# The last two sure expert steps add their rows up in PSUM by one-hot products, with the branch last, values from two spans and idle products at the start

## The chip, the cores and the metric

The kernel runs on one core of a Trainium2 chip. The metric is device time in microseconds (us) of one execution, the median of three runs. The profile is of one further execution, taken by the hardware profiler; its times are counted from the first instruction of the program. Engines are named as the profile names them: PE (TensorE, the matmuls; PEld its weight loads), DVE (VectorE), ACT (ScalarE), POOL (GpSimd) and SP (SyncE, which here only issues DMAs).

## What is computed

Two decoder layers on `x` of 4 sequences, 256 tokens, 256 features, with a context of 4 x 1601 rows, in float32. After each of six blocks the input is added and the sum goes through a layer normalisation.

```python
x = ln(x + L0_attention(x))        # 16 heads of 16, sliding window: 64 queries see 2 x 64 keys
x = ln(x + L0_cross(x, ctx))       # keys: 1601 of the context and the 256 tokens themselves
x = ln(x + L0_ffn(x))              # ternary weights, activations rounded to 8 bits
x = ln(x + L1_attention(x))        # causal, 16 heads, low-rank keys and values
x = ln(x + L1_cross(x, ctx))       # linear attention over the context
x = ln(x + L1_ffn(x))              # 8 experts, 2 per token
```

The last one concerns the end of the kernel:

```python
logits = 30 * tanh(x @ w_gate / 30); weights = softmax(logits), kept for the top 2 of 8 experts
for e in range(8):
    out += (silu(x @ w1[e]) * (x @ w3[e])) @ w2[e] * weights[:, e]
```

The first one concerns its start: each block of 64 queries sees its own 64 keys and the 64 before them, as far as these lie at a distance of 0 to 64.

## The kernel before, in words

**How the order is made.** The kernel doesn't issue instructions directly. Every call on `k` (a `Loom`) records an operation with an estimated cost per engine; a `piece` is a group of matmuls that stays together. At the end `weave()` (L317) is a list scheduler: it takes, over and over, the operation that can start first by its model, and emits it, so each engine has a fixed order in the finished program. Buffers belong to rings (`Group`), PSUM is one ring of eight banks (`psB`, tag `bank`), and a buffer comes free by the model's time. A change of one operation can thus move others on all engines. All DMAs of plain form go through SP in one order.

**The start.** SP loads the first sequence's `xT`, the query, key and value weights (`wqkv`) and the context of sequence 2. POOL meanwhile builds the identity, ones, the window mask `wmask`, the head mask `hmask` and two value buffers `v` (filled with zeros). `hmask` gives `qmask`, by which the keys are scaled.

**The first attention (`l0_attention`, L681).** Per sequence: products for keys and queries, then values in three spans of 128 tokens, at 0, 64 and 128 (`for i in range(3)`, L693), each two products of 128x256 whose outcome DVE and ACT copy into `v[:, i]`, the even and the odd heads. Tokens 0 to 127 as queries use span 0, tokens 128 to 191 span 1, tokens 192 to 255 span 2. `unit(j)` (two per sequence) makes scores for eight heads, adds the mask on DVE, takes the softmax on DVE and ACT (`softmax`, L643), turns the outcome on PE and multiplies by `v`. Between these the scheduler places matmuls of `context_sums`, which belong to the second layer's cross attention.

**The experts.** `route` picks two experts per token and POOL scatters the token's row, with its weight and its place, into a list per expert in DRAM (`lists`, filled with zeros before that by six DMAs in `moe_prepare`, L1231). `tile_table` works out on the core which 128 rows of which expert are the next tiles. An expert step, `expert_tile` (L1413), reads 128 rows (`xg`), loads that expert's `w1` and `w3`, turns the rows, makes 16 products for both matrices, applies the gate and makes four products with `w2` into `py`. DVE scales `py` to `y`, and POOL scatters the 128 rows of `y` to the DRAM array `yd`, which has two rows per token (`scatter`, L1262).

There are 23 tiles at most. 20 are always run; the last three (`RARE`) stand in a branch, `rare_tiles` (L1478), which is entered only if the tokens spread so that more tiles are needed. In the profiled execution it isn't. The branch stands after the sure steps and before the end. After it, per sequence, SP reads two blocks of `yd` back (`back`, a ring of four), DVE adds both to `x`, `normalise` (L614) takes statistics on DVE, the root on POOL and the scaling on DVE, and SP stores the sequence to `out` (L1576 to L1584).

Of the kernel before, what the change touches and what calls it, by code (L numbers as in the profile page):

```python
# [31 lines left out]
P = 128  # L32
# [105 lines left out]
class Pool:  # L138
# [3 lines left out]

    def tile(self, shape, dtype, tag, name=None, bufs=None, free=False, acc=False):
        if self.scope.loom.at_once is not None:
            return self.scope.loom.at_once[tag].pop(0)
        g = self.groups.get(tag)
        if g is None:
            g = self.groups[tag] = Group(self, tag, bufs or self.bufs, free)
        b = Buf(g, list(shape), dtype, name or tag, acc)
        self.scope.bufs.append(b)  # L150
        return View(b, None, shape)
# [281 lines left out]
def decoder(ctx: ExitStack, tc: tile.TileContext, a: dict, out: bass.AP):  # L433
# [44 lines left out]
    def tiny(shape, tag, dtype=F32):  # L478
        return small.tile(shape, dtype, tag, free=True)
# [70 lines left out]
    for b in range(1, B):  # L550
        load_x(b)
        load_res(b)

    ident = const.tile((P, P), F32, "ident")
    k.op({"POOL": (1.2, 1.2, lambda: make_identity(nc, ident.real()))}, [ident], [])
    identb = const.tile((P, P), BF16, "identb")
# [9 lines left out]
        )  # L566

    wmask = p1w.tile((P, 2, P), F32, "wmask")
    lower = p1.tile((P, 2, 2, P), F32, "at", bufs=7)[:, 0, 0]
    k.gpsimd.memset(wmask, 0.0)
    k.gpsimd.memset(lower, 0.0)
    for m, off in ((wmask[:, 0], 0), (wmask[:, 1], 64), (lower, 0)):
        keep_where(m, [[-1, P]], off, 1, NEG)
        keep_where(m, [[1, P]], 64 - off, -1, NEG)
    k.vector.tensor_copy(wmask[64:, 1], lower[64:])
# [7 lines left out]
    for par in range(2):  # L586
# [3 lines left out]
            axis=AX.X,  # L590
        )
    k.vector.tensor_scalar(qmask, qmask, 0.25, None, ALU.mult)


    vs = []
# [85 lines left out]
    def l0_attention(b):  # L681
# [20 lines left out]
        oT = pool.tile((P, 2, S), F32, "oT1", bufs=1)  # L702

        def unit(j):
# [512 lines left out]
    EARLY[1] -= EARLY[0]  # L1217
    TILES = 2 * T // P + NE - 1
    LATE = TILES - sum(EARLY)
    RARE = NE // 2 - 1  # L1220
    LISTS = (NE + 1) * T
    W = D + 2
# [8 lines left out]
    def moe_prepare():  # L1231
        pool, n = p5w, LISTS // P
        blank = p3.tile((P, FF), F32, "h")[:, :W]
        k.gpsimd.memset(blank, 0.0)
        for i in range(0, n, 12):
            dst = lists[i * P : (i + 12) * P, :].rearrange("(n p) w -> p n w", p=P)
            filled.append(k.dma_start(dst, blank.unsqueeze(1).to_broadcast([P, 12, W]), after=loaded))
        places = pool.tile((P, T // P, 2), F32, "places")
# [17 lines left out]
    filled, entered, taken_up, made = [], [], [], []  # L1256

    def apart(new, others):
        for o in others:
# [150 lines left out]

    tables = []

    def expert_tile(i, tab, level):  # L1413
        pool = p6
        reg = {}

# [46 lines left out]
        with piece(1.75, [y], ins=[w2], what="tile"):  # L1463
            for c in range(4):
# [2 lines left out]
                    c == 0, c == 3,  # L1467
                )
        k.also = [k.vector.tensor_scalar(y, py, gate, 0.5, ALU.mult, ALU.mult)]
        slots = p5.tile((P, 1), I32, "slots")  # L1470
# [7 lines left out]
    def rare_tiles(tiles, tab, more, level):  # L1478

        spare = [  # L1480
            p5.tile((P, W), F32, "xg"), p6w.tile((P, 2, 2, EI), F32, "wt"), p6.tile((P, 2, P), F32, "xgT"),
            p6.tile((P, EI // P, P), F32, "eh"), p6.tile((P, D), F32, "ey"), p5.tile((P, 1), I32, "slots"),
        ]
        banks = [bank((P, 2, P)), bank((P, EI // P, P)), bank((P, EI // P, P)), bank((P, D))]

        def emit():
            k.hold_order(False)
# [2 lines left out]
            for arm in tc.Switch(which, 2):  # L1490
                if arm:
                    for i in tiles:
                        k.at_once = {v.buf.group.tag: [v] for v in spare}
                        k.at_once["bank"] = list(banks)
                        expert_tile(i, tab, level)
                        k.at_once = None
            k.hold_order(True)

        k.op({None: (0.0, 2.5, emit)}, [yd], [tab, more, w2], [*spare, *banks], after=[o for o in k.ops if o.bufs], unordered=True)


    for b in range(B):
# [67 lines left out]
        X[b] = xn  # L1570
    at_prio(8)
    tab, more = tile_table(LATE, taken, True)
    for i in range(LATE - RARE):
        expert_tile(i, tab, level)
    rare_tiles(range(LATE - RARE, LATE), tab, more, level)
    for b in range(B):  # L1576
        x = X[b]
        for e in range(2):
            y = p6.tile((P, 2, D), F32, "back", bufs=4)
            row0 = 1 + e * T + b * S  # L1580
            k.dma_start(y, yd[row0 : row0 + S, :].rearrange("(t p) d -> p t d", p=P))
            k.vector.tensor_tensor(x, x, y, ALU.add)
        normalise(x)
        k.dma_start(out[b * S : (b + 1) * S, :].rearrange("(t p) d -> p t d", p=P), x)  # L1584
    k.weave()


# [69 lines left out]
```

## Time and profile before

| | us |
|---|---|
| median of three runs (lowest, highest) | 696.57 (695.5, 697.3) |
| the profiled execution | 696.37 |
| its span, first to last instruction | 694.7 |
| PE busy | 646.5 (93%) |
| DVE busy | 441.5 (64%) |
| ACT busy | 294.3 (42%) |
| POOL busy | 123.4 (18%) |
| DMA: read and written | 83.53 MB, mean 120 GB/s |

A busy share is that of an engine over the whole span, and matmuls overlap each other, so it doesn't say what a stage waits for. For that one reads a stage's own lines. In a line of the timeline the columns are the start, the length, the engine, the line of the code (a helper's, mostly), the operation, the tiles written and read, the number of instructions merged, and in brackets how long the engine had been idle and what released it. A record of PE is half a product in float32: two records stand for one 128x256 product.

### The profile page before, as it was taken

The numbers are of one execution on the slowest core, as the hardware profiler recorded it, in microseconds if no ns is written. First come the engines' busy times: TensorE is split into PE (matmuls) and PEld (weight loads), VectorE is DVE, ScalarE is ACT, GpSimd is POOL, SyncE is SP. The second block draws the span as 40 slices with busy tenths as digits, with TensorE's granted clock in tenths as the row PEclk, the third lists the DMA queues.
The fourth block names the chain that finished last, engine by engine and source line by source line (L and its number), as shares of the span: only waits on it lengthen the run. The fifth ranks groups of instructions, "written<-read, shape, count | busy, mean of one in ns | idle before, by whom it ended". The sixth has DMA issues, their size and how long they took to land.

```text
span 694.7 us, 12093 instructions
## 1 busy us (share of the span) xinstructions
PE 646.5 (93%) x4281; PEld 514.7 (74%) x4285; DVE 441.5 (64%) x1141; ACT 294.3 (42%) x924; POOL 123.4 (18%) x167
## 2 busy tenths in 40 slices
PE   7999999999999999999999999999997899999950
PEld 5787878668877777776667677777775799899940
DVE  5878897333527654374599997776688375333326
ACT  2767965211132433344346777656456312111100
POOL 3313223013300000000022101141203022111112
PEclk9999999999999999999999999999999899999985
DMA  9922100636998322000020330000000681996315
GB/s 303 357 83 77 41 31 1 212 93 231 330 300 293 122 95 94 1 1 0 1 55 1 105 139 1 1 30 1 31 1 23 218 288 43 330 308 235 116 45 168
DMA packets 60480, 83.53 MB, mean 120 GB/s; under 512 B 4462, under 2 KB 43764, under 8 KB 60404
## 3 DMA queue, kind: packets, MB, share of 16 engines
q1 hardware_dynamic: 58676, 77.86, 34.0%
q0 software_dynamic: 1728, 4.74, 1.9%
q8 instruction: 38, 0.62, 0.4%
q14 instruction: 38, 0.31, 0.2%
HBM read 67.29 MB, written 15.29 MB: 119 GB/s over the span
## 4 chain that ended last, share of the span: by engine, by line
PE 66%; DVE 14%; issue 11%; ACT 4%; POOL 3%; DMA 2%; SPq 0%; POOLq 0%; DVEq 0%
PE bank L269 58%; PE bank L276 8%; DVE at L406 4%; ACT at L406 3%; DVE nm L406 2%; POOL yd L1267 2%; DVE x L406 1%; DVE h L406 1%; POOL rstd L406 1%; DVE as L406 1%; DVE entry L406 1%; DVE st L406 1%; DMA yd<-ey,slots 1%; DVE kf L406 0%; DMA back<-yd 0%
## 5 line engine op out<-in xcount | busy, mean ns | idle before, releaser
L406 ACT ACTIVATE at<-at,nm 128x128 f32<-128x128 f32 (+1 forms) x256 | 106.5, 420 | 25.7 <-DVE nm L406 25.2
L269 PE MATMUL bank<-xgT,wt 128*128 128x128 f32 x640 | 75.9, 279 | 1.4 <-DMA wt<-in_w 0.9
L269 PEld LDWEIGHTS bank<-xgT,wt 128*128 128x128 f32 x640 | 75.1, 195 | 2.5 <-issue 1.3
L276 PE MATMUL bank<-ident,at 128*128 128x128 f32 (+1 forms) x440 | 61.4, 277 | 1.8 <-DVE at L406 1.6
L276 PEld LDWEIGHTS bank<-ident,at 128*128 128x128 f32 (+1 forms) x440 | 51.0, 142 | 13.8 <-issue 5.7
L269 PE MATMUL bank<-V,aT 128*128 128x256 f32 (+1 forms) x240 | 55.2, 380 | 0.7 <-DVE o L406 0.7
L269 PE MATMUL bank<-KT,qT 128*128 128x512 f32 (+1 forms) x128 | 54.0, 553 | 0.0
L269 PEld LDWEIGHTS bank<-V,aT 128*128 128x128 f32 (+1 forms) x240 | 45.2, 190 | 11.2 <-issue 3.6
L406 POOL TENSOR_SCALAR rstd<-mv 128x2 f32<-128x2 f32 (+1 forms) x26 | 6.5, 250 | 264.3 <-DVE mv L406 218.7
L269 PE MATMUL bank<-kf,V 128*128 128x256 f32 (+1 forms) x208 | 50.4, 383 | 1.1 <-DVE kf L406 1.1
L406 DVE TENSOR_REDUCE nm<-at 128x4 f32<-128x512 f32 (+1 forms) x64 | 50.7, 808 | 0.4
L269 PE MATMUL bank<-wkv,KT 128*128 128x256 f32 (+1 forms) x208 | 49.7, 382 | 0.0
L406 ACT ACTIVATION_READ_ACCUMULATOR at<-at,nm 128x1 f32 x256 | 48.8, 191 | 0.0
L406 ACT COPY aT<-bank 128x512 f32<-128x512 f32 (+2 forms) x60 | 31.4, 552 | 30.2 <-PE bank L276 29.5
L269 PEld LDWEIGHTS bank<-kf,V 128*128 128x128 f32 (+1 forms) x208 | 38.2, 190 | 7.5 <-DVE kf L406 2.3
L269 PEld LDWEIGHTS bank<-wkv,KT 128*128 128x128 f32 (+1 forms) x208 | 37.8, 186 | 7.3 <-issue 1.5
L406 ACT ACTIVATE eh<-bank 128x512 f32<-128x512 f32 x20 | 11.9, 597 | 67.9 <-PE bank L269 60.0
L406 DVE TENSOR_TENSOR at<-at,rs 128x512 f32<-128x512 f32 (+1 forms) x43 | 39.8, 925 | 0.8
L406 POOL TENSOR_TENSOR at<-at,rs 128x512 f32<-128x512 f32 (+1 forms) x21 | 23.5, 1121 | 86.9 <-DVE rs L406 73.6
L269 PE MATMUL bank<-w2e,eh 128*128 x160 | 37.8, 380 | 0.0
L406 ACT ACTIVATE fm<-bank 128x512 f32<-128x512 f32 (+2 forms) x33 | 18.1, 552 | 46.1 <-PE bank L269 46.1
L406 DVE TENSOR_REDUCE m<-bank 128x1 f32<-128x512 f32 (+1 forms) x32 | 20.5, 640 | 25.8 <-PE bank L269 25.6
(247 smaller groups left out, 1215.3 us busy)
## 6 DMA issues: line engine op xcount, KB each, us to landing
wt<-in_w SPq DMA_DIRECT2D x40, 512.0 KB
lists<-h SPq DMA_DIRECT2D x6, 1548.0 KB
KT<-in_ctxT SPq DMA_DIRECT2D x6, 1024.0 KB
V<-in_ctx SPq DMA_DIRECT2D x6, 1024.0 KB
w2e<-in_w SPq DMA_DIRECT2D x8, 512.0 KB
KT<-in_ctxT SPq DMA_DIRECT2D x6, 577.0 KB
V<-in_ctx SPq DMA_DIRECT2D x6, 512.0 KB
xg<-lists SPq DMA_DIRECT2D x20, 129.0 KB
```

What stands on the lines that cost most here:

```text
L269: lambda: self.nc.tensor.matmul(real(o), real(lhsT), real(rhs), start=real(start), stop=stop, **kw)
L276: fns.append(lambda: self.nc.tensor.transpose(real(o), real(x), real(ident)))
L406: return getattr(engine, method)(*[real(x) for x in args], **{k: real(x) for k, x in kw.items()})
L1267: d = nc.gpsimd.indirect_dma_start(out=dst.real(), out_offset=bass.IndirectOffsetOnAxis(ap=row.real(), axis=0), in_=src.real(), in_offset= ...
```

## The change

It has five parts.

1. **Idle products.** At the very start DVE writes a tile of zeros (from the ring of `qT`), PE makes eight bf16 products of 128x512 from it into a bank that nobody reads, and ACT takes an Exp of one column of it.
2. **Masks.** `hmask` and `qmask` are built before `wmask`. The second half of `wmask` is for swapped halves of the keys.
3. **Values from two spans.** Only the spans at tokens 0 and 128 are multiplied. `v[:, 1]` is put together from half of each: rows 64 to 127 of the first span and rows 0 to 63 of the second. Each span is thus copied twice, once whole and once in half, by DVE and by ACT. Scores for the queries 128 to 191 are made in two halves of 64 keys each, swapped likewise.
4. **Clearing.** `moe_prepare` fills the first 2048 token rows of `yd` with zeros by two more DMAs, because rows that are no longer scattered are still read.
5. **The end.** The last two of the 20 sure steps don't scatter. DVE compares the place of each row with a ramp of 1024 numbers (`iotaT`, made on POOL) and gets a one-hot tile `pick`; eight products per step, two per sequence, add the rows of `y` to four PSUM banks `acc`, one per sequence. The rest is read back from `yd` once the other 18 steps have scattered, added to `x` as before, and `x` is put into `acc` by products with the identity ("base"). `finish` normalises out of PSUM, one half of each sequence on DVE and the other on ACT, into buffers of the ring `back`, and stores. `rare_tiles` comes after that: if it is entered, it adds its tiles to `acc` and finishes again. The order that the scheduler makes on PE for the end is: the last step's four products with `w2`, eight one-hot products of the step before, base of sequences 0 and 1, one-hot of 0, base 2, one-hot of 1, base 3, one-hot of 2 and 3.

```diff
 def tile(self, ...):
     if self.scope.loom.at_once is not None:
-        return self.scope.loom.at_once[tag].pop(0)
+        ring = self.scope.loom.at_once[tag]
+        ring.append(ring.pop(0))
+        return ring[-1]
...
+    zeros = p1.tile((P, 512), BF16, "qT")
+    k.vector.memset(zeros, 0.0)
+    idle = bank()
+    with piece(3.4, what="idle"):
+        for i in range(8):
+            mm(idle, zeros[:, :P], zeros, i == 0, i == 7)
+    k.scalar.activation(zeros[:, :1], zeros[:, :1], AF.Exp)
...
-    k.gpsimd.memset(wmask, 0.0)
-    for m, off in ((wmask[:, 0], 0), (wmask[:, 1], 64), (lower, 0)):
+    k.gpsimd.memset(wmask[:, 0], 0.0)
+    for m, off in ((wmask[:, 0], 0), (lower, 0)):
         keep_where(m, [[-1, P]], off, 1, NEG)
         keep_where(m, [[1, P]], 64 - off, -1, NEG)
+    k.gpsimd.memset(wmask[:64, 1], NEG)
+    keep_where(wmask[:64, 1], [[1, P]], -1, -1, 0.0)
+    keep_where(wmask[:64, 1], [[-1, P]], 63, 1, 0.0)
...
-        for i in range(3):
+        for i in (0, 2):
             pv = bank((P, D))
             ...
-            k.vector.tensor_copy(v[:, i, :, 0, :16], heads[:, :, 0, :])
-            k.scalar.copy(v[:, i, :, 1, 16:], heads[:, :, 1, :])
+            part = slice(0, 64) if i else slice(64, P)
+            for rr, n in ((slice(0, P), i), (part, 1)):
+                k.vector.tensor_copy(v[rr, n, :, 0, :16], heads[rr, :, 0, :])
+                k.scalar.copy(v[rr, n, :, 1, 16:], heads[rr, :, 1, :])
...
-                for c in range(2):
+                for c, to, k0, n in ((0, 0, P, 64), (0, 64, 64, 64), (1, 0, P, P)):
                     for r, (rr, ps) in enumerate(zip(quarters, pss)):
                         mm(
-                            ps[64 * c : 64 * c + 64, 1],
+                            ps[64 * c : 64 * c + 64, 1, :, to : to + n],
                             qT[rr, j, P + 64 * c : P + 64 * c + 64],
-                            kT[rr, j, :, 64 + 64 * c : P + 64 + 64 * c],
+                            kT[rr, j, :, k0 : k0 + n],
...
+        for i in range(0, 2 * T // P, 8):
+            dst = yd[1 + i * P : 1 + (i + 8) * P, :].rearrange("(n p) w -> p n w", p=P)
+            cleared.append(k.dma_start(dst, blank[:, :D]..., after=loaded))
...
-    def expert_tile(i, tab, level):
+    def expert_tile(i, tab, level, into=None, first=False):
...
+        if into:
+            of = p5.tile((P, 1), F32, "of", bufs=2)
+            k.vector.tensor_scalar(of, slot, T + 0.5, -T, ALU.is_gt, ALU.mult)
+            k.vector.tensor_tensor(of, of, slot, ALU.add)
+            pick = pool.tile((P, T // P, P), F32, "pick", bufs=LAST_TILES)
+            k.vector.tensor_scalar(pick, iotaT..., of, None, ALU.is_equal)
+            for b in range(B):
+                with piece(0.87, what="add up"):
+                    for t in range(2):
+                        mm(into[b][:, t, :], pick[:, 2 * b + t, :], y, first and t == 0, True, ...)
+            return
...
-        scatter(yd, slots, y, 1.0, 2.0, "give")
+        scatter(yd, slots, y, 1.0, 2.0, "give", cleared)
+
+    def finish(acc):
+        for b in range(B):
+            mv = tiny((P, 2, 2), "mv2")
+            o = p6.tile((P, 2, D), F32, "back", bufs=4)
+            for t in range(2):
+                st = tiny((P, 6), "st")
+                k.vector.bn_stats(st, acc[b][:, t, :])
+                k.vector.bn_aggr(mv[:, t, :], st)
+            rstd = tiny((P, 2), "rstd2")
+            k.gpsimd.tensor_scalar(rstd, mv[:, :, 1], 1e-5, None, ALU.add)
+            k.gpsimd.tensor_tensor(rstd, rstd, mhalf, ALU.pow)
+            nmr = tiny((P, 1), "nmr")
+            k.vector.scalar_tensor_tensor(nmr, mv[:, 1, 0:1], -1.0, rstd[:, 1:2], ALU.mult, ALU.mult)
+            k.vector.tensor_scalar(o[:, 0], acc[b][:, 0], mv[:, 0, 0:1], rstd[:, 0:1], ALU.subtract, ALU.mult)
+            k.scalar.activation(o[:, 1], acc[b][:, 1], AF.Identity, scale=rstd[:, 1:2], bias=nmr)
+            k.dma_start(out[b * S : (b + 1) * S, :].rearrange("(t p) d -> p t d", p=P), o)
...
-    for i in range(LATE - RARE):
-        expert_tile(i, tab, level)
-    rare_tiles(range(LATE - RARE, LATE), tab, more, level)
-    for b in range(B):
-        ...                                  # reload, add, normalise, store
+    acc = [bank((P, 2, D)) for _ in range(B)]
+    sure = LATE - RARE
+    for i in range(sure):
+        last = i - sure + LAST_TILES
+        if last < 0:
+            expert_tile(i, tab, level)
+        else:
+            expert_tile(i, tab, level, acc, last == 0)
+        if last == 0:
+            for b in range(B):
+                x = X[b]
+                for e in range(2):
+                    y = p6.tile((P, 2, D), F32, "back", bufs=4)
+                    row0 = 1 + e * T + b * S
+                    k.dma_start(y, yd[row0 : row0 + S, :].rearrange("(t p) d -> p t d", p=P))
+                    k.vector.tensor_tensor(x, x, y, ALU.add)
+                with piece(0.87, what="base"):
+                    for t in range(2):
+                        mm(acc[b][:, t, :], ident, x[:, t, :], False, True, skip_group_check=True)
+    finish(acc)
+    rare_tiles(range(sure, LATE), tab, more, level, acc)
```

More of the change, by code (lines that the diff above doesn't have):

```diff
@@ L566, in keep_where @@
         )
-    wmask = p1w.tile((P, 2, P), F32, "wmask")
-    lower = p1.tile((P, 2, 2, P), F32, "at", bufs=7)[:, 0, 0]
-    k.gpsimd.memset(wmask, 0.0)
-    k.gpsimd.memset(lower, 0.0)
-    for m, off in ((wmask[:, 0], 0), (wmask[:, 1], 64), (lower, 0)):
-        keep_where(m, [[-1, P]], off, 1, NEG)
-        keep_where(m, [[1, P]], 64 - off, -1, NEG)
-    k.vector.tensor_copy(wmask[64:, 1], lower[64:])
     hmask = const.tile((P, 8, 17), F32, "hmask")
@@ L592, in decoder @@
     k.vector.tensor_scalar(qmask, qmask, 0.25, None, ALU.mult)
+    wmask = p1w.tile((P, 2, P), F32, "wmask")
+    lower = p1.tile((P, 2, 2, P), F32, "at", bufs=7)[:, 0, 0]
+    k.gpsimd.memset(wmask[:, 0], 0.0)
+    k.gpsimd.memset(lower, 0.0)
+    for m, off in ((wmask[:, 0], 0), (lower, 0)):
+        keep_where(m, [[-1, P]], off, 1, NEG)
+        keep_where(m, [[1, P]], 64 - off, -1, NEG)
+    k.gpsimd.memset(wmask[:64, 1], NEG)
+    keep_where(wmask[:64, 1], [[1, P]], -1, -1, 0.0)
+    keep_where(wmask[:64, 1], [[-1, P]], 63, 1, 0.0)
+    k.vector.tensor_copy(wmask[64:, 1], lower[64:])
     vs = []
@@ L1219, in decoder @@
     LATE = TILES - sum(EARLY)
+    LAST_TILES = 2
     RARE = NE // 2 - 1
@@ L1237, in moe_prepare @@
             filled.append(k.dma_start(dst, blank.unsqueeze(1).to_broadcast([P, 12, W]), after=loaded))
+        for i in range(0, 2 * T // P, 8):
+            dst = yd[1 + i * P : 1 + (i + 8) * P, :].rearrange("(n p) w -> p n w", p=P)
+            cleared.append(k.dma_start(dst, blank[:, :D].unsqueeze(1).to_broadcast([P, 8, D]), after=loaded))
         places = pool.tile((P, T // P, 2), F32, "places")
@@ L1254, in moe_prepare @@
         return places, ahead, onesb, spare, iotaN, start, nxt
-    filled, entered, taken_up, made = [], [], [], []
+    filled, cleared, entered, taken_up, made = [], [], [], [], []
     def apart(new, others):
@@ L1469, in expert_tile @@
         k.also = [k.vector.tensor_scalar(y, py, gate, 0.5, ALU.mult, ALU.mult)]
+        if into:
+            k.also = []
+            of = p5.tile((P, 1), F32, "of", bufs=2)
+            k.vector.tensor_scalar(of, slot, T + 0.5, -T, ALU.is_gt, ALU.mult)
+            k.vector.tensor_tensor(of, of, slot, ALU.add)
+            pick = pool.tile((P, T // P, P), F32, "pick", bufs=LAST_TILES)
+            k.vector.tensor_scalar(pick, iotaT.unsqueeze(1).rearrange("p o (n q) -> p (o n) q", q=P), of, None, ALU.is_equal)
+            for b in range(B):
+                with piece(0.87, what="add up"):
+                    for t in range(2):
+                        mm(into[b][:, t, :], pick[:, 2 * b + t, :], y, first and t == 0, True, skip_group_check=True)
+            return
         slots = p5.tile((P, 1), I32, "slots")
@@ L1475, in expert_tile, with rare_tiles @@
         k.vector.tensor_tensor(slots, slots, slot, ALU.add)
-        scatter(yd, slots, y, 1.0, 2.0, "give")
-    def rare_tiles(tiles, tab, more, level):
-        spare = [
-            p5.tile((P, W), F32, "xg"), p6w.tile((P, 2, 2, EI), F32, "wt"), p6.tile((P, 2, P), F32, "xgT"),
-            p6.tile((P, EI // P, P), F32, "eh"), p6.tile((P, D), F32, "ey"), p5.tile((P, 1), I32, "slots"),
-        ]
-        banks = [bank((P, 2, P)), bank((P, EI // P, P)), bank((P, EI // P, P)), bank((P, D))]
+        scatter(yd, slots, y, 1.0, 2.0, "give", cleared)
[15 more added lines that the diff above has]
+            k.dma_start(out[b * S : (b + 1) * S, :].rearrange("(t p) d -> p t d", p=P), o)
+    def rare_tiles(tiles, tab, more, level, acc):
+        spare = {}
+        for v in (
+            p5.tile((P, W), F32, "xg"), p6w.tile((P, 2, 2, EI), F32, "wt"), p6.tile((P, 2, P), F32, "xgT"),
+            p6.tile((P, EI // P, P), F32, "eh"), p6.tile((P, D), F32, "ey"), p5.tile((P, 1), F32, "of", bufs=2),
+            p6.tile((P, T // P, P), F32, "pick", bufs=LAST_TILES), p6.tile((P, 2, D), F32, "back", bufs=4),
+            tiny((P, 2, 2), "mv2"), tiny((P, 6), "st"), tiny((P, 2), "rstd2"), tiny((P, 1), "nmr"),
+            bank((P, 2, P)), bank((P, EI // P, P)), bank((P, EI // P, P)), bank((P, D)),
+        ):
+            spare.setdefault(v.buf.group.tag, []).append(v)
         def emit():
@@ L1492, in emit @@
                     for i in tiles:
-                        k.at_once = {v.buf.group.tag: [v] for v in spare}
-                        k.at_once["bank"] = list(banks)
-                        expert_tile(i, tab, level)
-                        k.at_once = None
+                        k.at_once = spare
+                        expert_tile(i, tab, level, acc)
+                    finish(acc)
+                    k.at_once = None
             k.hold_order(True)
-        k.op({None: (0.0, 2.5, emit)}, [yd], [tab, more, w2], [*spare, *banks], after=[o for o in k.ops if o.bufs], unordered=True)
+        k.op({None: (0.0, 2.5, emit)}, [*acc], [tab, more, w2], [v for vs in spare.values() for v in vs], after=[o for o in k.ops if o.bufs], unordered=True)
     for b in range(B):
@@ L1572, in decoder @@
     tab, more = tile_table(LATE, taken, True)
-    for i in range(LATE - RARE):
-        expert_tile(i, tab, level)
-    rare_tiles(range(LATE - RARE, LATE), tab, more, level)
-    for b in range(B):
[L1577 to L1584, printed above, removed]
+    iotaT = p6.tile((P, T), F32, "iotaT", bufs=1)
+    iota(iotaT, 1, base=1)
+    acc = [bank((P, 2, D)) for _ in range(B)]
[17 more added lines that the diff above has]
+                        mm(acc[b][:, t, :], ident, x[:, t, :], False, True, skip_group_check=True)
+    finish(acc)
+    rare_tiles(range(sure, LATE), tab, more, level, acc)
     k.weave()
```

## The prediction

> **What bounds the kernel now.** I read the busy table by slice first, then the busy times stage by stage, then the two ends of the timeline, since the change works at both ends and in the first attention.
>
> From the page, the 40 equal slices:
>
> ```profile
> PE   7999999999999999999999999999997899999950
> DVE  5878897333527654374599997776688375333326
> DMA  9922100636998322000020330000000681996315
> ```
>
> TensorE is full in nearly every slice but the first, two near 530 us and the last two. By stage (columns: us, then busy us and records of PE, weight loads, DVE, ACT, POOL):
>
> ```profile
> 0.00:107.00 107.00, 100.61 (x957) 81.42 (x958) 87.26 (x189) 74.77 (x303) 29.55 (x47) 1.00 0.44 145
> 107.00:350.00 243.00, 240.62 (x1214) 179.66 (x1214) 124.25 (x296) 77.73 (x190) 24.92 (x28) 1.00 0.40 127
> 540.00:669.00 129.00, 125.20 (x929) 117.88 (x927) 58.35 (x209) 23.28 (x54) 24.89 (x29) 0.98 0.59 207
> 669.00:694.70 25.70, 0.00 (x0) 0.00 (x0) 11.73 (x35) 0.00 (x0) 5.34 (x9) 0.59 0.45 137
> ```
>
> Of the 6.4 us that PE is idle before 107 us, 4.36 are the wait for the first weights, so a matmul less in the first attention is time less. The last 25.7 us hold no matmul at all. The head in time order:
>
> ```profile
> 4.36 5.51 PE L269 MATMUL bank<-xt,wqkv 128*128 128x256 f32 x16 [4.36 <-DMA wqkv<-in_wqkvT]
> 7.03 1.28 ACT L406 ACT_TABLE_LOAD   x1 [7.03 <-DVE qmask L406]
> 9.70 2.75 PE L269 MATMUL bank<-wqkv,xt 128*128 128x256 f32 x12
> 12.39 1.33 PE L269 MATMUL bank<-kT,qT 32*128 32x256 f32 x24
> 30.15 2.75 PE L269 MATMUL bank<-wqkv,xt 128*128 128x256 f32 x12
> 32.74 1.89 PE L269 MATMUL bank<-xt,wqkv 128*128 128x256 f32 x8
> ```
>
> One product of 128x256 in f32 is two records. From 30.15 to 32.74 twelve records pass in 2.59 us, 0.216 each (0.432 a product). The first sixteen need 5.34 us (4.36 to 9.70), not 3.46: 1.88 us of slow start. The tail:
>
> ```profile
> 662.72 0.96 POOL L1267 DMA_INDIRECT yd<-ey,slots  x1 [7.92 <-DVE slots L406]
> 669.74 0.96 POOL L1267 DMA_INDIRECT yd<-ey,slots  x1 [0.77 <-DVE slots L406]
> 674.85 7.73 SPq L283 DMA_DIRECT2D back<-yd  x8
> 678.47 0.69 DVE L406 TENSOR_TENSOR entry<-entry,back 128x512 f32<-128x512 f32 x1 [9.00 <-DMA back<-yd]
> 690.12 0.74 DVE L406 TENSOR_SCALAR entry<-entry,mv,rstd 128x256 f32<-128x256 f32 x2 [0.28 <-POOL rstd L406]
> ```
>
> After the last matmul (668.69) come in series: the last scatter, 4.95 us on the chain of waits (669.74 to 674.69), eight reloads and adds to 687.88, normalising to 690.86, and 3.84 us of store and end.
>
> [...] at twice 0.216 for slow records, 1.88 us is 8.7 slow ones, 3.75 us. (The granted clock stands at 1.00 there, so that column doesn't show it.) [...] Here twenty scatters of 128 KB land 2.4, 3.1 (median) and 5.0 us after issue.
>
> **Part by part. Head.** DVE writes the zeros at about 0.8 to 1.1 us. The eight bf16 products of 512 columns are as long as eight f32 records of 256 (0.216 warm: the layer-0 feed-forward has them), 0.43 at half rate, 3.46 together: about 1.2 to 4.7. So the first real product starts 0.3 late[...]. If all sixteen records are then fast, they end at 8.2, not 9.7: +1.5. Bounds: -0.3 ([...] all slow) and +1.9. I take 1.4. The Exp on the zeros moves the 1.28 us table load into ACT's empty first 7 us. The head mask now comes first on POOL; key scaling (ACT 0.69, then DVE 0.75 after the k products) ends near 7.9, before the scores near 9.9. Both are worth 0 themselves, since PE waited for neither, but without them the scores would start at 9.8 at the earliest. The window mask, behind both 1.38 us fills on POOL, is done near 7.6; its first reader comes at 11. Cost 0.
>
> **Values from two spans.** One of three spans goes per sequence: two products, 0.865, times four: 3.46 us of PE. Added: one copy on DVE (0.277) and one on ACT (0.262) per sequence, 1.1 us on each in a stage where they are busy 87 and 75 of 107; hidden by PE. The split scores have the same columns (256 as twice 128). Four row tiles side by side pass 256 columns in 0.216, so 128 in 0.108; the smallest records here (48 of aT,v in 1.02 us, 0.021 each, 0.085 for four) lie under that. So 0, at most 0.4 in all. I take 3.3.
>
> **Clearing.** Two more DMAs of 1.05 MB on SP behind the six of the lists: those move 9.5 MB between 169.78 and 196.65, so 2.1 MB take 5.9 us. Behind them wait the feed-forward weights and the next context. But the queue gets there some 4.7 us earlier, so they come 1.2 later on the clock; the reduction of the late weight starts at 212.3, 10.7 after its issue ended, and PE's product that needs it now stands some 7 us of matmuls later. Cost 0. Uncovered, it is 5.9.
>
> **Reordered first half.** The scheduler's new order differs on PE up to about 350 us. PE idles only 8.8 us there, head included; I allow 0.5 lost (-1.5 to +2).
>
> **Tail.** The last two sure steps give up their scatter; the last one left is that of 662.72, landing at 665.8 to 667.7 (I take 666.5). The eight reloads then go while PE still works. In the trace the first add starts 3.6 after the first issue, the next 0.85 apart; the ring holds four, so reloads five to eight are issued only after an add (4.4, 5.2, 6.05, 7.4 after the first) and land 3.1 later. Last add done 11 us after the landing: 677.5. PE's order after its last expert product is eight one-hot products (668.69 to 672.15), base of sequences 0 and 1 (their adds done 671.7 and 673.4; PE to 674.4), one-hot 0 (675.2), base 2 (add 675.6; to 676.6), one-hot 1 (677.4), base 3 (to 678.5), one-hot 2 and 3 (680.2). So the 24 products (10.4 us) carry 1.1 us of waits. Then for sequence 3: DVE half a microsecond behind, statistics 0.75 and 0.2, POOL 1.1, factor and first half on DVE 0.6, then ACT's half 0.56 (it waits for that DVE pair): 684.0. Then 3.84 as before and 0.4 for the branch, which now stands last on every engine, the order being such that SP passes it only after the stores land: 688.3. Gain 6.4. Bounds: scatter landing at 667.7 gives 5.2; PE never waiting 7.5; a branch that costs 2 leaves 4.8. The one-hot tiles themselves (DVE, two of about 0.75) and the 1024-long ramp (POOL, near 1 us between its norms at 542.5 and 548.7) are hidden: DVE is busy 58 of 129 there.
>
> **Sum.** 1.4 + 3.3 - 0.5 + 6.4 = 10.6. The profiled execution is 696.37 (span 694.7 and 1.67 around it), 0.2 under the median of 696.57: 685.8.
>
> **Rivals.** *Only the tail counts (690.0).* The softmax chain on DVE and ACT takes up what PE saves early. For it: between 66 and 107 us the chain of waits runs through many of their pieces, DVE near 90% busy from 60 to 80. Against: PE is busy 59.76 of the 60 us from 40 to 100. Chance 0.15.
>
> *The tail stays serial (688.9).* The scatter takes 4.95, and branch and barrier 2: the gain is 6.4 - 1.2 - 1.6 = 3.6, less 0.3 of DVE queueing. For it: the last scatter did take 4.95. Against: two were then close together (668.02, 669.74), and 662.72 stands alone. Chance 0.13.
>
> *Slower (697.6).* The clears stop PE twice, at the weight sums near 215 us and at the next context: 2 x 5.9 = 11.8 lost against 10.6 won. It decides from 10.6 us of new PE waits between 200 and 300 us, where PE has none now. Against: a DVE wait of 1.1 us on such a weight is all that the trace has there. Chance 0.04.
>
> *More (682.5).* PE never waits in the tail, [...] and the new order closes a gap (+2). Chance 0.08.
>
> **How the numbers follow.** The forecast, 684 to 688, has 0.60. 682 to 690 takes in most of the first two rivals and the low side; what is left out is the slower case, half of the first rival and a little below: under 0.2. Faster by over 0.3% (2.1 us, about what a measurement of this kernel tells from no change): 0.95; same 0.01; slower 0.04.
>
> **What would show it.** Right: the v products at about 8.2 us; no third span; PE full to 107 us less about 4.7; 24 products after the last expert product with PE waits of 1 to 2 us on DVE's adds; first reload issued before PE's last expert product ends; nothing of the scatter on the chain behind it. Wrong: slow records still after 5 us; new PE waits on raw or KT near 200 to 300 us; base products waiting over 3 us; over 5 us from the last store's issue to the end.

## The result, and the profile after

The changed kernel takes 690.15 us (median of 6 runs, 687.6 to 691.83) against 696.43 for the kernel before beside it (6 runs, 695.5 to 697.3): 6.3 us less, ratio 0.9909 with a 95% interval of 0.9888 to 0.9929. The forecast was 685.8 us with a range of 682 to 690, so the gain has the right sign and is 4.3 us short. The profiled execution took 690.3 us with a span of 688.6; the one of before 696.37 and 694.7. The traces differ by 6.1 us, and the question is where the other 4 went.

First the page of the kernel after: PE's busy time in 40 equal slices (tenths):

```profile
PE   9999999999999999999989999999997899999992
```

PE now works in the whole first slice, and the last two, which were 5 and 0, are 9 and 2. By stage (columns as in the table of before: from and to, us, busy us and records of PE, weight loads, DVE, ACT, POOL, then granted clock, DMA share, GB/s):

```profile
0.00:107.00 107.00, 103.03 (x1033) 82.04 (x1034) 91.23 (x196) 75.47 (x305) 29.77 (x47) 1.00 0.46 151
...
669.00:688.60 19.60, 6.00 (x28) 4.95 (x26) 7.75 (x27) 2.25 (x4) 3.69 (x8) 0.73 0.27 85
```

The timeline of the kernel after at both ends (start, us, engine, line, operation, out<-in, count, and in brackets the idle time before it and what ended it):

```profile
1.25 3.60 PE L271 MATMUL bank<-qT 128*128 128x512 bf16 x8 [1.25 <-DVE qT L408]
...
4.64 4.04 PE L271 MATMUL bank<-xt,wqkv 128*128 128x256 f32 x16
...
8.53 1.89 PE L271 MATMUL bank<-wqkv,xt 128*128 128x256 f32 x8
...
10.35 1.36 PE L271 MATMUL bank<-kT,qT 32*128 32x256 f32 x32
...
661.02 3.62 PE L271 MATMUL bank<-w2e,eh 128*128 x16
661.23 6.97 SPq L285 DMA_DIRECT2D back<-yd  x8
...
667.93 1.89 PE L271 MATMUL bank<-entry,ident 128*128 128x256 f32 x8
...
673.11 1.89 PE L271 MATMUL bank<-ey,pick 128*128 128x256 f32 x8
...
678.88 0.56 ACT L408 ACTIVATE back<-bank,nmr,rstd 128x256 f32<-128x256 f32 x1 [0.42 <-DVE back L408]
```

The first scores come at 10.35 us, not 12.39. PE's last product with `w2` ends at 664.64 (661.02 + 3.62), not 668.69: 4.05 less. From there to the last half of `finish` on ACT (679.44) it is 14.8 us. All of this is close to the forecast. What is not is the rest: from 679.44 to the end of the span at 688.6 pass 9.15 us. In the kernel before it was 3.84.

What is there? The queue instructions of the branch and of the end of the kernel after (line 1548 is the `Switch`, line 1722 what closes the program; columns: count, duration in ns as min/median/max, first and last start):

```profile
L1548 SPq EVENT_SEMAPHORE  x9: 17/17/17, 680.7 to 684.2; - x9
```

```profile
L1722 SPq EVENT_SEMAPHORE  x14: 17/28/28, 686.9 to 688.5; - x14
...
L1722 PEldq COMPARE_BRANCH  x2: 351/2010/3670, 672.2 to 675.3; - x2
...
L1722 SPq COMPARE_BRANCH  x2: 42/50/58, 680.1 to 684.2; - x2
L1722 DVEq DRAIN  x2: 10/29/48, 684.1 to 688.0; - x2
```

SP issues its last store at 679.47, passes into the empty arm, and there waits for the stores; its last wait ends at 684.0. It then jumps over the other arm: the branch itself stands at 684.24 for 0.06 us, but SP's next instruction starts at 686.92, 2.68 us later. DVE jumped at 679.20 and did its next thing at 684.12. And the stores are late. The instructions that write `out`, with the time from issue to landing:

```profile
L285 SPq DMA_DIRECT2D out<-back x4: 372/375/378, 675.4 to 679.5; - x4
...
DMA to landing us min/median/max: 3.2/4.1/4.5
```

Between 678 and 689 us the DMA queues of the kernel after move not only the stores (queue, kind, packets, MB, share of 16 engines):

```profile
q1 hardware_dynamic: 663, 0.63, 19.0%
q14 instruction: 12, 0.10, 3.1%
q8 instruction: 1, 0.02, 0.6%
```

Thirteen packets of 8 or 16 KB of instructions run there. Nine start between 678.7 and 682.4 us, while the stores are on their way. Three start between SP's branch and SP's next instruction, at 684.7 to 685.2, and in the stretch from 684.2 to 687 us nothing else is moved at all:

```profile
q14 instruction: 3, 0.02, 3.0%
```

In the last 5 us of the kernel before there was one such packet, after the stores. So two things stand beside these packets: a jump after which SP does nothing for 2.68 us, and stores that take up to 4.5 us to land. Whether the packets cause either, one profile doesn't show. The runs were made to tell these two from a plain slow end.

### The profile page after: what moved, and what is told of

Its sections match the earlier page's. It is cut to its first block, busy times and chain, and to the rows that moved or that the text cites. A ratio compares the mean times of both kernels' runs of the same rounds, so it can differ in the third digit from the quotient of the medians.

```text
span 688.6 us, 12316 instructions
## 1 busy us (share of the span) xinstructions
PE 656.5 (95%) x4385; PEld 524.3 (76%) x4389; DVE 444.0 (64%) x1152; ACT 296.2 (43%) x930; POOL 120.7 (18%) x166
## 4 chain that ended last, share of the span: by engine, by line
PE 83%; DVE 10%; ACT 4%; POOL 1%; issue 1%; ACTq 0%; POOLq 0%; DVEq 0%
PE bank L271 74%; PE bank L278 9%; ACT at L408 3%; DVE at L408 2%; DVE nm L408 2%; DVE x L408 1%; POOL rstd L408 1%; DVE st L408 0%; DVE h L408 0%; DVE fm L408 0%; DVE as L408 0%; DVE kf L408 0%; ACT fm L408 0%; DVE back L408 0%; DVE bank L408 0%
## 5 line engine op out<-in xcount | busy, mean ns | idle before, releaser
L408 DVE TENSOR_TENSOR at<-at,rs 128x512 f32<-128x512 f32 (+1 forms) x44 | 38.4, 873 | 1.0
L408 POOL TENSOR_TENSOR at<-at,rs 128x512 f32<-128x512 f32 (+1 forms) x20 | 22.8, 1141 | 87.9 <-DVE rs L408 80.7
```

Source lines behind the costliest of these rows:

```text
L408: return getattr(engine, method)(*[real(x) for x in args], **{k: real(x) for k, x in kw.items()})
```

## The experiments

The times below stand beside runs of the kernel before on the same chip. Those chips took 699.5 to 700.0 us for it, not 696.4, which is itself one of the questions; ratios are compared, not times of different chips.

### The branch taken out

```diff
-    rare_tiles(range(sure, LATE), tab, more, level, acc)
```

> The changed kernel without its last operation, the branch to the three rare tiles (left out: those tiles, which these inputs do not need). Theory A (the branch at the end costs about 5 us, of which 2.7 is the jump on SP over the arm not taken and some 2.3 the late landing of the last stores, which share the DMA engines with the instructions being fetched): from the last ACT half to the end 3.8 us as in the kernel before, against 9.15 in the changed kernel, so a span near 683.3 and a time near 685.0 us. The last store lands 2.2 us after its issue, not 4.5. Theory B (the branch costs the 0.4 of the forecast; the stores are late because four of them, and the reloads, now stand close together): the last store still lands about 4.5 us after issue, time 689.7. Theory C (only the jump): 687.4, the last store landing at 4.5.

684.15 us (683.73 to 686.19), ratio 0.9785 (0.9754 to 0.9817). The changed kernel itself, run again without any edit, gives the base:

> The changed kernel once more, unaltered, so that the three beside it have their base on the same chip. Both theories: 9.1 us from the last ACT half to the end as in its first profile, the last store landing 4.5 us after its issue. If the late landing was an accident of that one profile (theory B), it lands within 2.5 us of its issue here and 7 us remain.

689.89 us (689.78 to 693.62), ratio 0.9859 (0.9838 to 0.9880); from the last ACT half (682.64) to the end (691.90) 9.26 us, the last store landing 4.76 after its issue. The late landing comes again, so it is no accident of one profile. Without the branch, in the view of what writes `out`:

```profile
L285 SPq DMA_DIRECT2D out<-back x4: 372/375/378, 677.2 to 681.3; - x4
...
DMA to landing us min/median/max: 2.1/2.1/2.1
```

and its DMA queues from 680 us on:

```profile
q1 hardware_dynamic: 577, 0.54, 32.0%
```

No packet of instructions moves, the stores land in 2.1 us, and from the last ACT half (681.23) to the end (684.46) it is 3.23. Theory A holds, B and C do not: with the branch gone, the stores land early and the end is short. The branch costs 5.9 us of the span between the last ACT half and the end. The ratios, 0.9859 and 0.9785, differ by 0.0074, which is 5.2 us of 700; the medians by 5.7, but on two chips. Of the 5.9, 2.4 are the late stores (4.55 against 2.14), 2.7 the jump on SP, and 0.8 the semaphores of the empty arm and a longer row of them at the end.

### The branch taken out of the kernel before

```diff
-    rare_tiles(range(LATE - RARE, LATE), tab, more, level)
```

> The kernel before without the branch (left out: the three rare tiles, not needed on these inputs). Theory A (there the jumps were hidden behind the landing of the last scatter, but the instructions fetched for them held that scatter up): the scatter lands 3.1 us after its issue, the median of the others, not 4.95, and the time falls by 1.9 to 694.5 us. Theory B (the scatter was slow on its own account, since two stand 1.7 us apart): no difference, 696.4. Either way the 3.84 us from the last DVE work to the end stay.

696.13 us, ratio 0.9950 (0.9935 to 0.9966): 3.5 us less. So the branch was not free there either. The last scatter and the first reload after it:

```profile
672.84 0.96 POOL L1267 DMA_INDIRECT yd<-ey,slots  x1 [0.76 <-DVE slots L406]
675.37 4.97 SPq L283 DMA_DIRECT2D back<-yd  x6
```

The scatter lands in 2.4 us, and the reload starts 2.5 us after the scatter's issue, not 5.1 (674.85 less 669.74). Here too two scatters stand 1.7 us apart (671.11 and 672.84), so theory B is out. In the five profiles with the branch in its old place the last scatter took 3.9 to 5.6 us. From the last `w2` product to the end it is 22.8 us against 26.0 in the first profile of before and 26.4 in a later one. That is more than the 1.9 expected: the scatter gained 2.5, and the last DVE work stands 0.45 nearer to the end. The old place hid the jumps but not the late scatter. In the first profile of before six packets of instructions (four of 8 KB, two of 16) start while that scatter is on its way; that they held it up is the author's reading of this pair of runs, as with the stores, and isn't shown apart from the jumps.

### The arms swapped

```diff
-    k.vector.tensor_scalar(more, ..., ALU.is_gt)
+    k.vector.tensor_scalar(more, ..., ALU.is_le)
...
-                if arm:
+                if not arm:
                     for i in tiles:
```

> The changed kernel with the two arms of the branch in the other order: the rare tiles first, the empty arm second, so that an engine that does not take the rare tiles jumps where it enters the branch and then runs on into the end. Theory A (the 2.7 us jump on SP stands in series behind the wait for the stores because the empty arm lies ahead of the other): SP jumps at 680.1, while the stores fly, finds them landed at about 684.0, and the end comes 1.8 later: span 685.9, time 687.5 us, 2.7 less than the changed kernel's 690.2. Theory B (a jump is needed at the entry and another at the end of the arm, or the jump is not what takes those 2.7 us): 690 us or more. Theory C (stores late only because of fetched instructions, which here are fewer since one jump does for two): down to 685.5.

689.93 us, ratio 0.9867 (0.9835 to 0.9898), beside 0.9859 for the changed kernel: no difference. In the trace SP takes 2.77 us to enter (681.88 to 684.65) and again 1.60 to leave (685.40 to 687.00); DVE 3.32 and 3.06. From the last ACT half to the end it is 8.19, 0.9 less than in the changed kernel, in one profile. Theory B: also the arm that is last, with nothing behind it to be jumped over, ends in a jump, after which SP does nothing for 1.60 us.

### Both arms empty

```diff
                 if arm:
-                    for i in tiles:
-                        k.at_once = spare
-                        expert_tile(i, tab, level, acc)
-                    finish(acc)
-                    k.at_once = None
+                    pass
```

> The changed kernel with the branch kept but nothing in either arm (left out: the three rare tiles, which these inputs do not need, and the second normalising in that arm). Theory A [...]: with the end right behind the branch the jump is short; from the last ACT half to the end 3.2 us as without a branch and at most 1 more, the last store landing 2.2 us after its issue; 5 us less than the changed kernel beside it. Theory B (a jump costs 2.7 us on SP however short it is): the stores land in 2.2 to 2.5 us, the jump stays, 2 to 2.5 us less than the changed kernel.

695.84 us, ratio 0.9942 (0.9923 to 0.9960): 6 us more than the changed kernel, where both theories had 2 to 5 less. An empty branch writes nothing, so the scheduler was free to move it forward, and in the trace it stands among the expert steps near 595 us. The kernel thus measured something else: the stall of a branch in the middle of work. Its timeline on PE there:

```profile
595.99 0.38 PE L278 MATMUL bank<-ident,xg 128*128 128x128 f32 x2
...
606.14 2.26 PE L271 MATMUL bank<-xgT,wt 128*128 128x128 f32 x9 [9.76 <-issue]
```

PE stands for 9.8 us with nothing that it waits for. Its two branch instructions, into the arm and out of it:

```profile
L1718 PEldq COMPARE_BRANCH  x2: 4648/4964/5281, 595.5 to 601.0; - x2
```

What the way in, 5.28 us, holds isn't shown (the reading of the condition stands right before it here); the way out, 4.65, is a jump over an arm with nothing in it. The other engines needed 5.7 to 6.3 us for that jump, from 592.4 us on. So, as theory B has it, a jump over an empty arm is not short. On PE this is clean: its way out begins at 601.03, with the DMA engines nearly idle (busy share 0.13 and 0.37 in the next two microseconds), and 4.65 us lie near the 4.27 and 3.67 that PE's jump over a full arm takes in the first profiles of before and after. For the other four engines it isn't, because they jumped while the DMA engines were full. In the table by stage (columns as above):

```profile
592.00:598.00 6.00, 4.03 (x34) 3.82 (x34) 0.00 (x0) 0.60 (x1) 0.89 (x1) 1.00 1.04 382
```

The DMA share (the last column but one) is 1.04, mostly weights of the next steps, and the first packet of instructions starts only at 595.46, 3 us after DVE's jump. So how long their jump takes by itself isn't shown. And the end of this kernel, with no branch there, is as that of the kernel without one: stores land in 2.1 us, 3.26 from the last ACT half to the end.

### The branch ahead of the normalising

```diff
-                    finish(acc)
                     k.at_once = None
...
-    finish(acc)
     rare_tiles(range(sure, LATE), tab, more, level, acc)
+    finish(acc)
```

> The changed kernel with the normalising and the stores behind the branch (once for both arms) and only the rare tiles in the arm. Theory A (a jump costs only where nothing covers it): DVE reaches the branch at 671.9 after its last add and passes it 4.9 us later at 676.8, while PE still sums; four sequences' statistics and halves then take 6.5 (7.6 in the changed kernel, of which 1.1 are waits for PE), and the end follows 3.3 after that as without a branch: span 686.6, time 688.3, 1.9 less than the changed kernel. Theory B (the branch costs its 5.9 wherever it stands): no difference, or slower because DVE no longer overlaps PE: 690 to 693.

689.74 us (688.07 to 690.36), ratio 0.9846 (0.9822 to 0.9869): not to be told from the changed kernel's 0.9859. The end is short again (3.67, stores in 2.2 us), and from the last `w2` product to the end it is 22.9 us, against 23.9 and 25.0 in the two profiles of the changed kernel. Most of the branch's price went elsewhere. In its timeline, DVE:

```profile
673.02 1.42 DVE L408 TENSOR_TENSOR entry<-entry,back 128x512 f32<-128x512 f32 x2 [1.14 <-SPq L1548]
...
678.16 0.76 DVE L408 BATCH_NORM_STATS2 st<-bank 128x6 f32<-128x256 f32 x2 [3.73 <-PEq L1548]
```

The last two adds wait 1.14 us for SP, which passes on the reloads' semaphores in its empty arm, and the statistics start at 678.16, 3.4 us after DVE's own jump began, not at 676.8. After them `finish` can no longer overlap PE. Theory A gave the mechanism right and the sum 1 to 2 us too good.

### The branch one expert step earlier

```diff
         if last == 0:
+            rare_tiles(range(sure, LATE), tab, more, level, acc)
             for b in range(B):
...
-    finish(acc)
-    rare_tiles(range(sure, LATE), tab, more, level, acc)
+    finish(acc)
```

> The changed kernel with the branch one expert step earlier (before the last sure step, with only the rare tiles in the arm; the normalising and the stores stand at the end, once). Theory A: PE pays its own jump, 3.7 us with nothing to do, and DVE 4.9, in place of the 5.9 at the end: 2.2 less to 1 more than the changed kernel, 688 to 691. Rival: SP jumps ahead of the gather and the weights of the last step, which come later by its jump and the waits in the empty arm; if they are needed at once PE waits 5 to 10 us more, 693 to 700.

694.82 us, ratio 0.9922 (0.9901 to 0.9944): 4.4 us more than the changed kernel by the ratios. Its waits on PE from 640 us on:

```profile
PE bank L278 <- issue: 5.6, 1, 5.6
PE bank L271 <- DVE ey L408: 1.2, 2, 0.6
```

PE stops once for 5.6 us, with no wait for weights: the rival's mechanism is absent although its number fits. Theory A had the mechanism and missed what follows the stop: 32 products of the next step take 4.84 us instead of 3.73 and four base products' records 0.43 each instead of 0.22; PE's records are slow until 674.5 (granted clock 0.50 from 670 to 674). DVE's `pick` for the step before comes only at 665.31, after DVE's own jump. The stop (5.6), the slow records (an estimate from their lengths: 2.2) and the two waits (1.2), less what the end gains (9.26 to 3.67 us), are 3.4 of the 4.4; the rest is open.

### First half alone

```diff
+    zeros = ...; idle products; Exp; head mask first; new window mask
+    values from two spans; scores in three parts
     # no clearing; scatters, reloads and branch as before
```

> The kernel before with the first half of the change alone: idle products, Exp and mask order at the head, and values from two spans with split scores; no clearing, and the old tail with scatters, reloads and the branch ahead of them. Theory A (the steps add up as forecast): 1.4 + 3.3 - 0.5 (another order on PE) = 4.2 us less, 692.2 us. Rival (the first half yields only the idle products and the spans are taken up by DVE and ACT): 695.0. If the order of the scheduler decides, any value between 690.7 and 694.2.

693.08 us, ratio 0.9921 (0.9892 to 0.9951): 5.5 us less, with an interval from 3.4 to 7.6. The profiles show how much of it is the edit's. Against the kernel before on a later chip (its second profile, below) 4.6 us are won up to the last `w2` product (666.71, not 671.27) and 1.8 in the old tail, which this kernel has unaltered: its last scatter landed 3.9 us after its issue, not 5.4. The 4.6 fits theory A's 4.2; the rival's 1.4 is out.

### Spans alone, clearing alone, and the kernel before again

Spans alone leave the head as it was, and also the old window mask, which doesn't fit the swapped keys. The values computed from there on are wrong; the trace has the same 20 sure steps and doesn't enter the rare tiles.

```diff
-        for i in range(3):
+        for i in (0, 2):
...
-                for c in range(2):
+                for c, to, k0, n in ((0, 0, P, 64), (0, 64, 64, 64), (1, 0, P, P)):
```

> The kernel before with the values from two spans and the split scores alone. Theory A (PE is full in the first attention, so 3.46 us of products less are 3.3 less): 3.3 us less than the kernel before beside it, within 1.5 for another order on PE: 696.5. Rival (DVE and ACT, which get a copy more per sequence, take it up): 0 to 1 us less.

693.75 us, ratio 0.9907 (0.9878 to 0.9936): 6.5 us less, 3.2 more than the term and outside theory A's 1.5 for another order. Clearing alone:

```diff
+        for i in range(0, 2 * T // P, 8):
+            dst = yd[1 + i * P : 1 + (i + 8) * P, :].rearrange("(n p) w -> p n w", p=P)
+            cleared.append(k.dma_start(dst, blank[:, :D]..., after=loaded))
```

> The kernel before with the two clearing DMAs added and nothing else (nothing reads their zeros there). Theory A (2.1 MB more on SP behind the lists, hidden): no difference, within 1 us for another order. Rival (what queues behind them comes 5.9 us later and PE waits once): 5.9 us more; twice: 11.8.

696.58 us, ratio 0.9953 (0.9922 to 0.9984): 3.3 us *less*. More work, less time. The kernel before, unaltered, says in part why:

> The kernel before, unaltered, to find where the 3.4 us lie that it takes more on the later chips (699.6 to 700.0) than in its first times (696.4), which the changed kernel does not. Theory A (they lie in the head and in the last scatter, which hang on when data arrive): first weights near 5.2 us and a dozen slow records where the first profile had 4.36 and eight, the scores 1.8 later at 14.2; the last scatter lands 5 to 7 us after its issue, not 4.95; the stages between as before. Theory B (TensorE's clock is granted less over the whole): scores at 12.4, and a shift that grows evenly to 3 us by 660.

699.52 us, ratio 0.9996 to the other runs of it. Its waits on PE, with one that the first profile does not have:

```profile
PE bank L269 <- DVE wabs L406: 1.8, 1, 1.8
```

and the view of the tile `wabs`, the reduction of the late feed-forward weight:

```profile
L406 DVE TENSOR_REDUCE wabs<-raw x3: 2276/2276/2286, 176.7 to 215.0; 128x1 f32<-128x2048 f32 x3
...
  DMA raw<-in_w0dT: 2.6, 1
```

The weight comes 2.7 us later than in the first profile (the reduction starts at 215.0, not 212.3; between 160 and 220 us the DMA engines move 288 GB/s, not 297), DVE waits 2.6 us for it and PE 1.8 to 2.2. The two theories both fail: the scores come at 12.48, as in the first profile (12.39), and the difference does not grow evenly. From the first score to the last `w2` product it is 658.8 us against 656.3, and that one wait is most of it. The other three kernels without the clearing that ran on these chips have it too (the one without a branch 1.6 us, spans alone 1.4, the first half alone 1.3). In the kernels with the clearing the scheduler puts other products ahead of the one that needs `wabs` (217.9 us in the kernel after, 223.3 with clearing alone), and PE does not wait. So on those chips the change gains some 2 us from an order that nobody asked for. That is about half of the difference between the 10 us that it gains there (ratio 0.9859) and the 6.3 on the chip of the result; the other half stays open. More of the same kind shows between the single edits. From the first score to the last `w2` product, clearing alone takes 654.0 us and spans alone 654.5, with 2.6 us less of products only in the second. And from the last `w2` product to the end, which neither edit touches, it is 27.2 and 24.8 us. The order that the scheduler makes and the landing of the last scatter thus move a time by about 2 us each, so an edit alone doesn't give the price of an edit.

### More idle products

```diff
-        for i in range(8):
-            mm(idle, zeros[:, :P], zeros, i == 0, i == 7)
+        for i in range(13):
+            mm(idle, zeros[:, :P], zeros, i == 0, i == 12)
```

on top of the branch ahead of the normalising.

> The changed kernel with the normalising and the stores behind the branch, as in the earlier run, and thirteen idle products in place of eight. Theory A (the idle products end at 4.65 us while the weights arrive anywhere from 4.4 to 5.7; [...] the first profiles had 0 to 8 slow records after it): five more end near 5.7, no real record is slow, the scores start at 10.9 us at the latest: 0.5 to 1 less than with eight, 689.0. Rival (a real product that could have begun at 4.4 now waits until 5.7 or later): 0.5 to 1 more.

689.06 us (688.29 to 689.57), ratio 0.9839 (0.9815 to 0.9863), beside 0.9846 with eight: no difference. No real record is slow, as expected, but eleven of the thirteen idle ones are, the first real one starts at 6.41, and the scores at 11.69, not 10.9. That is the rival's mechanism, a real product that waits for idle ones, without its price of 0.5 to 1 us. Of all these kernels none that keeps the rare tiles is measurably better than the changed one.

## Why the prediction was wrong

**Head: right, with luck in the size.** Forecast 1.4 (bounds -0.3 to 1.9). In the kernel before PE's first nine records start 0.43 us apart on average (4.36 to 8.19), those after them 0.22; in the kernel after the eight idle ones and the first two real ones start 0.43 apart (1.25 to 5.50), the next 0.22. The granted clock is 1.00 in both stretches. So in this profile the idle products stood in for slow records; that they would was the author's estimate. The first real product starts at 4.64, 0.3 late as said; the products of `v` come at 8.53, not 8.2, because two real records were still slow. The scores come 2.04 us earlier, of which 0.86 are the two products of the first sequence that are gone (four records of 0.216): 1.2 for the head. In the second profile of the same kernel the first real product starts at 5.67, eight real records are slow, and the scores come at 12.76: no gain against 12.39. The size hangs on chance on both sides: in the eight profiles with eight idle products (the changed kernel twice, and the runs without a branch, with it swapped, empty, ahead or early, and the first half alone) 0 to 8 real records were slow and the scores came between 10.35 and 12.76; in those without, 7 to 14 were slow. The first real product starts anywhere from 4.36 to 5.67, and an unbroken stretch of slow records lasts 3 to 6 us. Why the number of slow records changes from run to run isn't shown.

**Values from two spans: right as a mechanism; the size of 3.3 isn't shown by itself.** No third span is left, PE has 103.03 busy us before 107, 3.4 of them idle products, where it had 100.61. After the start it waits there for the same three tiles as before, none more than 0.4 us longer. The split scores pass in 1.28 us where they took 1.26. What the rival "only the tail counts" needed, DVE and ACT taking up the gain, did not happen: the first half alone gains 4.6 us up to the last `w2` product.

**Clearing: right in the profile, with a hidden gain elsewhere.** No DMA of `raw` or `KT` is among PE's waits after the change. What the prediction noted as cover, that PE's product which needs the late weight stands some 7 us of matmuls later, is on other chips worth 2 us by itself.

**Reordered first half: right**, as far as the sum goes. 1.4 + 3.3 - 0.5 = 4.2 was forecast to the last `w2` product, 4.05 measured. With orders and heads that move by 2 us from kernel to kernel and from run to run, so close a hit is in part luck.

**Tail up to the last half: right.** The forecast's times stand on the clock of before, so 4.05 comes off them. First reload issued at 661.23, before PE's last expert product ends (forecast 662.4, after the landing of the scatter); last add done at 671.83 (673.4); 24 products after the last expert product, done at 675.0 (676.1); the last ACT half done at 679.44 (679.95). From the last `w2` product that is 14.8 us where 15.3 was forecast. Nothing of a scatter is on the chain of waits.

**The end: here it failed.** The step is "0.4 for the branch, which now stands last on every engine". It measured 5.3: 9.15 from the last half to the end, less the 3.84 of before. Against an end with no branch at all (3.23) it is 5.9. With 5.3 in place of 0.4 the sum would have been a gain of 5.7 and 690.7 us; measured were 690.15. The 0.4 came from no line of the trace. The bound beside it, a branch that costs 2, had no row behind it either, and the sign named for it, "over 5 us from the last store's issue to the end", is what came: 9.1. Three things were left out. The jump out of the empty arm is not 0.05 us of an instruction but 2.7 us on SP (2.9 to 4.9 on the others) until the next one starts. It stands behind the wait for the stores, which SP passes in the empty arm. And the stores land 2.4 us later (4.55 against 2.14), while nine packets of instructions start in the DMA queues.

Could it have been read? Yes, in the kernel before, in the same view:

```profile
L1653 ACTq COMPARE_BRANCH  x2: 43/50/58, 663.7 to 664.3; - x2
...
L1653 PEldq COMPARE_BRANCH  x2: 2820/3547/4274, 666.8 to 670.1; - x2
L1653 ACTq DRAIN  x2: 8/44/81, 667.1 to 694.1; - x2
```

ACT jumps at 664.30 and its next instruction, with no wait that the profile shows, starts at 667.11: 2.8 us. PE's branch at 670.11 lasts 4.27. ACT's jump lay under PE's last products (to 668.69) and PE's under the landing of the last scatter (669.74 to 674.69), and that cover is what the change takes away when it moves the branch to the end. What holds an engine in such a gap isn't shown; in SP's 2.68 us of the kernel after three packets of 8 KB of instructions start. A jump over an empty arm stalled as well: 4.7 us on PE, and 5.7 to 6.3 on the others while the DMA engines were full.

**The rivals.** "Only the tail counts" has the number (690.0) but not the mechanism: the first half paid 4.05 of its 4.2, and the tail paid less. "The tail stays serial" has a part of the cause, a branch and barrier of 2 us, but in its main part, a scatter of 4.95 us, it was wrong: the scatter lands before PE's last expert product ends. The 4.95 of the old tail came with the branch: without it, it is 2.4. So the price that the tail's gain removed and the price that it brought were two faces of one thing, 3.1 us before (25.97 less 22.84 from the last `w2` product to the end) and 5.9 after.

## What to carry to other kernels

A runtime branch cost an engine 1.6 to 6.3 us at the way out here, with a full arm and with an empty one to jump over, and transfers that ran beside packets of instructions landed late (stores in 3.2 to 5.3 us, not 2.1 to 2.3). So look at what lies beside it: under a landing that was waited for anyway it cost 3.1 us, at the end of the program, bare behind the last store, 5.9. When an edit moves a branch, a wait or a barrier, price it from the trace by the gap to the next instruction on its engine, not by the length of its own record.

And when a scheduler orders the work, test an edit together with the order that it gets: here a useless pair of DMAs made the kernel 3.3 us faster (1.1 to 5.5).

## What the runs showed that was not expected

- The branch instruction on SP, DVE, ACT and POOL has a record of 0.04 to 0.08 us, and the next instruction starts 1.6 to 6.3 us later; only PE's record holds the time (at the way out 4.27 in the first profile of before, 3.67 in that of after, 4.65 with empty arms). In the views of waits and of the timeline this time is "issue", if it is there at all.
- A store of 256 KB lands in 2.1 to 2.3 us where the branch is gone or stands earlier, and in 3.2 to 5.3 among some ten packets of instructions, most of 8 KB, though all of these are only a sixth of the bytes moved then (0.12 of 0.74 MB, from 678 to 689 us in the kernel after). That they do it is argued from their coming and going together with the late landing; no run had them without jumps.
- Swapped arms cost two slow jumps where one was expected, and save nothing.
- Copies at 288 instead of 297 GB/s go with a stop of PE of 1.8 us in the kernel before. In the first profile the product that needs the weight's sums stood only 0.5 us behind their reduction (215.13 after 214.58).
